# Conditioned transformer block on one core: how the ff MLP's gates reach all partitions

## The chip, the cores and the metric

The kernel runs on one core of a Trainium2 chip. The metric is the device time of one execution in microseconds. The core has five engines with a queue of instructions each: TensorE (PE in the profile, its weight loads PEld), VectorE (DVE), ScalarE (ACT), GpSimd (POOL), and SyncE (SP), which in this kernel only issues DMAs. Each works through its own queue in order, and waits where it needs another's result.

## The reference

Two batch entries of 2048 rows and 512 columns go through an MLP with exact gelu (512 to 512 to 512) and one with tanh gelu (512 to 1024 to 512). Each is wrapped in a layer norm with shift and scale, and in a gated residual sum; the six vectors (shift, scale and gate of either MLP) come from a condition, one row per batch entry.

```python
emb = jnp.dot(jax.nn.silu(t), ada_w) + ada_b            # t: (2, 512), emb: (2, 3072)
shift_msa, scale_msa, gate_msa, shift_mlp, scale_mlp, gate_mlp = jnp.split(emb, 6, axis=-1)
norm = _ln(x) * (1.0 + scale_msa[:, None]) + shift_msa[:, None]
h = jax.nn.gelu(jnp.dot(norm, ssm_w1) + ssm_b1, approximate=False)
x = x + gate_msa[:, None] * (jnp.dot(h, ssm_w2) + ssm_b2)
norm2 = _ln(x) * (1.0 + scale_mlp[:, None]) + shift_mlp[:, None]
hf = jax.nn.gelu(jnp.dot(norm2, ff_w1) + ff_b1, approximate=True)
x = x + gate_mlp[:, None] * (jnp.dot(hf, ff_w2) + ff_b2)
```

All of it is in float32. The change concerns gate_mlp, the sixth part of emb (index 5); gate_msa, the third part (index 2), is the ssm gate.

## The kernel before

**Tiling.** The 4096 rows are cut into eight blocks of 512 (128 partitions times 4 rows); blocks 0 to 3 belong to batch entry 0, blocks 4 to 7 to entry 1. Each block goes through a first product of the ssm MLP (hA_i), its second product (oA_i), a first product of the ff MLP (hC_i) and its second (oC_i).

**Products.** A product is cut into quarters and done in seven smaller products P1 to P7 in place of eight (`group`, L368 on); sums of quarters of the operands (nS, hSA, hSC, w_s, fw_s) go in, and each result is taken out of PSUM by VectorE or ScalarE. P1, P6, P7 and P4 add up in one PSUM bank (y), P5 and P3 in another (v), and P2 has a third (x). P6 may thus start only when P1's sum is taken out, P7 after P6's, P4 after P7's, P3 after P5's. The order is P1, P2, P6, P5, P7, P3, P4, in some groups with P5 ahead of P6 (`FIRST`). From block 1 on hC_i is done in 26 products of a list written out by hand (`HK_P`).

**Order.** The schedule is manual. Work of the other engines is hung as hooks behind the products of a group: each engine gets its instructions in the order in which the program issues them, and that is the order of the hooks.

**The norm's way.** x is normalized on ScalarE (`normal`, L465), turned in 32x32 squares on VectorE (`turn`, L476), moved between partitions by 16 DMAs (`move`, L485), modulated with shift and scale on ScalarE (`modulate`, L508), and its sums nS are made on GpSimd or VectorE (L311). For block 0's second norm eight of the moves are issued by SP within hA_1 and eight by ScalarE behind hA_1.

**The gates.** `rows_of_gates(g)` makes the rows of a gate for both batch entries by four column-tiled products of 512 columns (L284), one for each 128 of the 512 condition values, so that four partial sums stand in four partition groups; VectorE adds the bias row (brows) to them (L293, grows). `make_gate(g, b)` multiplies these with `pick_bc`, a matrix of ones at the rows of entry b: the product (L299, pgate) adds the four partial sums and puts the row on all 128 partitions of a PSUM tile at once. The gate is then folded into the second weight (`weight_of_second`, L359: w2 or fw2 times the gate, one of the K slices per operation) and into its bias row (gb: L830, L869, L632). The bias row is added to x on GpSimd ahead of the residual sum (`biases`, L625).

**Where the ff gate stands.** `rows_of_gates(5)` is a hook of P6 in hA_1, `make_gate(5, 0)` a hook of P3 there; gb's multiplication (gb5_0) and three of the four additions gb5 stand at P1 of oA_1, the folds of fw2 from P7 of oA_1 to hA_2. For entry 1, after oC_3, fw2 is loaded again and `make_gate(5, 1)` follows; its folds are hooks of block 4. The small loads of brows are issued on ScalarE's queue at the start, one row for each gate.

Of the kernel before, what the change touches and what calls it, by code (L numbers as in the profile page):

```python
# [36 lines left out]
F32 = mybir.dt.float32  # L37
AF = mybir.ActivationFunctionType
ALU = mybir.AluOpType
# [101 lines left out]
def kernel(  # L141
# [16 lines left out]
    nc = tc.nc  # L158
    P = 128
    B, N, D = x.shape  # L160
    H = fw1.shape[1]
    KD = D // P
    KH = H // P
    C = 4
# [3 lines left out]
    PER_B = N // TB  # L168
# [4 lines left out]
    sums = ctx.enter_context(tc.tile_pool(name="sums", bufs=4))  # L173
    work = ctx.enter_context(tc.tile_pool(name="work", bufs=1))
    small = ctx.enter_context(tc.tile_pool(name="small", bufs=3))
    ps_t = ctx.enter_context(tc.tile_pool(name="ps_t", bufs=2, space=bass.MemoryType.PSUM))
    ps_g = ctx.enter_context(tc.tile_pool(name="ps_g", bufs=2, space=bass.MemoryType.PSUM))

# [6 lines left out]
    G = 32  # L185
# [7 lines left out]
    def big_tile(name):  # L193
        return big.tile([P, KD, D], F32, tag="big", name=name)
# [9 lines left out]
    ada = {}  # L204

    def load_ada(g):
        ada[g] = big_tile(f"ada_{g}")
        nc.sync.dma_start(
            out=ada[g], in_=ada_w[:, g * D : (g + 1) * D].rearrange("(k p) n -> p k n", p=P)
        )  # L210

    def load_w(name, w, t=None, eng=nc.sync):
        if t is None:
            t = const.tile([P, w.shape[0] // P, w.shape[1]], F32, tag=name, name=name)
        eng.dma_start(out=t, in_=w.rearrange("(k p) n -> p k n", p=P))
        return t

    def load_row(t, row):
        nc.sync.dma_start(out=t, in_=row.unsqueeze(0).to_broadcast([P, D]))
        return t  # L220


    brows = big_tile("brows")
# [11 lines left out]
    w1_sb = load_w("w1", w1)  # L235
    load_ada(2)

    nc.gpsimd.memset(brows[:, :2, :], 0.0)
    for n, g in enumerate((2, 5)):
        nc.scalar.dma_start(  # L240
            out=brows[:B, n, :], in_=ada_b[g * D : (g + 1) * D].unsqueeze(0).to_broadcast([B, D])
        )
    w2_sb = load_w("w2", w2)
    b2_bc = work.tile([P, D], F32, tag="gb", name="gb2_0", bufs=2)
    load_row(b2_bc, b2)
# [4 lines left out]

    mods = {}

    def modulation(g0, part):


        g = g0 + part
        pa = ps_g.tile([P, D], F32, tag="x", name=f"pada_{g}")
        w = ada[g].rearrange("p k (n m q) -> p k m n q", n=KD, q=G)
        for k in range(KD):
            for m in range(P // G):  # L260
                nc.tensor.matmul(
                    pa[m * G : (m + 1) * G, :P],
                    silu[:, k, :],
                    w[:, k, m],
                    start=(k == 0),
                    stop=(k == KD - 1),
                    tile_position=(0, m * G),
                    skip_group_check=True,
                )
        turned = pa[:, P : 2 * P]  # L270
        nc.vector.transpose(turned, pa[:, :P])
        turned = turned.rearrange("p (n q) -> p n q", n=KD)
        m = const.tile([P, KD, B], F32, tag=f"mod_{g0}_{part}", name=f"mod_{g0}_{part}")
        bias = colsT[:, R_ADA + g * KD : R_ADA + (g + 1) * KD]
        nc.vector.tensor_tensor(m, turned[:, :, :B], bias.unsqueeze(2).to_broadcast([P, KD, B]), ALU.add)
        mods[g0, part] = m

    gate, gate_rows = {}, {}

    def rows_of_gates(g):  # L280

        pa = ps_g.tile([P, D], F32, tag="x", name=f"pada_{g}")
        for k in range(KD):
            nc.tensor.matmul(  # L284
                pa[k * G : (k + 1) * G, :],
                silu[:, k, :],
                ada[g][:, k, :],
                start=True,
                stop=True,
                tile_position=(0, k * G),  # L290
            )
        r = work.tile([P, D], F32, tag="grows", name=f"grows_{g}", bufs=2)
        nc.vector.tensor_tensor(r, pa, brows[:, (2, 5).index(g), :], ALU.add)  # L293
        gate_rows[g] = r

    def make_gate(g, b):

        pg = ps_t.tile([P, D], F32, tag="t", name=f"pgate_{g}_{b}")
        nc.tensor.matmul(pg, pick_bc[:, b, :], gate_rows[g], start=True, stop=True)  # L299
        gate[g, b] = pg  # L300


    def quarters(lo, hi, a, b):
# [36 lines left out]
    def weight_of_first(name, w_sb):  # L340

        K, M = w_sb.shape[1], w_sb.shape[2]
        tile_s = const.tile([P, 3, K // 2, M // 2], F32, tag=f"{name}_s", name=f"{name}_s")
        s = thirds(tile_s)
        lo, hi = w_sb[:, : K // 2, :], w_sb[:, K // 2 :, :]
        q = quarters(lo, hi, slice(0, M // 2), slice(M // 2, M))
        return first_operands(q, s), sums_of_first(q, s, nc.gpsimd), tile_s
# [58 lines left out]
    def hook(hooks, places, ops):  # L406

        for n, op in enumerate(ops):
            hooks.setdefault(places[min(n, len(places) - 1)], []).append(op)
# [212 lines left out]
    def biases(i, gb):  # L622

        return [
            lambda c=c: nc.gpsimd.tensor_tensor(xs[i][:, c, :], xs[i][:, c, :], gb, ALU.add)  # L625
            for c in range(C)
        ]
# [128 lines left out]
    n1 = {0: Norm(0, 1), 1: Norm(1, 1)}  # L756
# [42 lines left out]
    pick_bc = const.tile([P, B, P], F32, tag="pick_bc", name="pick_bc")  # L799
# [3 lines left out]
    w1_ops, w1_sums, _ = weight_of_first("w1", w1_sb)  # L803
# [14 lines left out]
    n1_sums = n1[0].summed(nc.vector)  # L818
    run(n1_sums[:2])
    load_ada(5)  # L820
    fw2_sb = load_w("fw2", fw2)
    gb, hA = {2: b2_bc}, {}
    found = {}

    def ssm_gate():
        make_gate(2, 0)
        found["w2"] = weight_of_second(w2_sb, w2_s, gate[2, 0], (nc.vector,))

    def gb2_0():
# [4 lines left out]

    hooks = {}
    hook(hooks, ("P1",), n1_sums[2:3])
    hook(hooks, ("P2",), [lambda: rows_of_gates(2)] + n1_sums[3:])
    st = n1[1].stats()
    hook(hooks, ("P5",), [ssm_gate, gb2_0] + biases(0, b2_bc) + fold2(0, 1))
    hook(hooks, ("P6",), fold2(1, 7))  # L840
# [5 lines left out]
    hA_sums = hA[0].summed(nc.vector)  # L846
    run(hA_sums[:2])
    hooks = {}
# [4 lines left out]
    n2 = {0: Norm(0, 2)}  # L853
    st = n2[0].stats()
    hook(hooks, ("P3",), st[:2])
    fw1_ops, fw1_sums, fw1_s = weight_of_first("fw1", fw1_sb)
# [2 lines left out]
    residual("oA_0", 0, hA[0], w2_ops, KD // 2, hooks, order=FIRST)  # L859

    def ff_gate():
        make_gate(5, 0)
        found["fw2"] = weight_of_second(fw2_sb, fw2_s, gate[5, 0], (nc.vector,), 4)

    def fold5(lo, hi):
        return [lambda k=k: found["fw2"][1][k]() for k in range(lo, hi)]
# [5 lines left out]
    n1_sums = n1[1].summed(nc.vector)  # L872
    run(st[2:3] + n1_sums[:2] + st[3:])
    hooks = {}
    hook(hooks, ("P1",), n1_sums[2:3] + [n2[0].scales])
    hook(hooks, ("P2",), n1_sums[3:] + [lambda c=c: n2[0].normal(c) for c in range(C)])
    hook(hooks, ("P2",), biases(1, gb[2]))
    hook(hooks, ("P6",), [lambda: rows_of_gates(5)])
    hook(hooks, ("P6", "P6", "P7", "P7"), [lambda c=c: n2[0].turn(c) for c in range(C)])
    hook(hooks, ("P7",), [lambda: n2[0].move((nc.sync,), (0, 1))])  # L880
    hook(hooks, ("P3",), [ff_gate])
    fb2_bc = work.tile([P, D], F32, tag="gb", name="gb5_0", bufs=2)
    load_row(fb2_bc, fb2)
    load_x(2)
# [6 lines left out]
    hA_sums = hA[1].summed(nc.vector)  # L891
# [2 lines left out]
    st = n1[2].stats()  # L894
    hooks = {}
    gb5 = biases(0, gb[5])
    hook(hooks, ("P1",), hA_sums[2:3] + [gb5_0] + fw1_sums[3:] + gb5[:3])
    hook(hooks, ("P2",), hA_sums[3:])
    hook(hooks, ("P2", "P6", "P6", "P5"), st)
    hook(hooks, ("P6",), n2[0].moved())  # L900
    n2_sums = n2[0].summed(nc.gpsimd)
    hook(hooks, ("P5",), n2_sums[:1] + [n1[2].scales])
    hook(hooks, ("P7",), n2_sums[1:] + [lambda c=c: n1[2].normal(c) for c in range(C)] + gb5[3:])
    hook(hooks, ("P7", "P3", "P4"), fold5(0, 3))
    turns = [lambda c=c: n1[2].turn(c) for c in range(C)]
    residual("oA_1", 1, hA[1], w2_ops, KD // 2, hooks)
# [2 lines left out]
    hC = Second(0)  # L909
    n2[1] = Norm(1, 2)  # L910
    hooks = {}
    hook(hooks, ("P1",), biases(2, gb[2]))
    hook(hooks, ("P1", "P1", "P2"), turns)
    hook(hooks, ("P2",), [n1[2].move])
    hook(hooks, ("P6", "P5", "P7", "P3"), n2[1].stats())
# [21 lines left out]
    hooks = {}  # L937
# [10 lines left out]
    hooks = {}  # L948
# [6 lines left out]
    hooks = {}  # L955
# [11 lines left out]
    for i in range(1, NBLK):  # L967
        nxt, nx2, last = i + 1 < NBLK, i + 2 < NBLK, i + 1 == NBLK
        hC = Second(i)
        hooks = {}  # L970
        if i == 1:
            hook(hooks, range(0, 26), take(len(fa_sums)))
        if i == 1:
            hook(hooks, (0,), [n1[i + 2].scales])
        if nxt:
            hook(hooks, (1, 2, 3, 4), hA[i + 1].summed(nc.gpsimd))
        hook(hooks, (6, 7, 8, 9), biases(i, gb[5]))
# [3 lines left out]
            hook(hooks, (20,), [n1[i + 2].move])  # L981
        if fold:
            hook(hooks, (2, 6, 23, 25), fold[:4])
        hook(hooks, (20,), hC.summed(0, nc.gpsimd))
        hC.products(fa, fb[i], hooks, last or i == 1)

        hooks = {}
# [16 lines left out]
        hooks = {}  # L1004
# [14 lines left out]
        if refold2:  # L1019
            b = (i + 2) // PER_B  # L1020
            gb[2], multiply_2 = gate_bias(2, b, b2, f"gb2_{b}")
            hook(hooks, ("P1",), [lambda: load_w("w2", w2, w2_sb)])
        if nx2:
            if refold2:
                hook(hooks, ("P1",), [lambda: make_gate(2, b)])
                hook(hooks, ("P6",), [multiply_2])
            hook(hooks, ("P1", "P2"), n1[i + 2].summed(nc.gpsimd))
            hook(hooks, ("P6",) if refold2 else ("P2", "P6"), biases(i + 2, gb[2]))
# [5 lines left out]
        if refold5:  # L1034
            b = (i + 1) // PER_B
# [22 lines left out]

        if refold5:
            load_w("fw2", fw2, fw2_sb)  # L1060
            make_gate(5, b)
            fw2_ops, fold = weight_of_second(fw2_sb, fw2_s, gate[5, b], (nc.vector,))
        hooks = {}
        if refold5:
# [51 lines left out]
```

## Time and profile before

| | |
|---|---|
| time, median of 3 runs | 600.43 us (600.42 to 600.75) |
| the profiled execution's own time | 600.48 us |
| its span, first to last instruction | 598.7 us |
| granted TensorE clock, mean | 0.999 |
| HBM read, written | 25.72 MB, 8.39 MB |
| ff gate's products, L299, each | 0.86 us on the chain, two of them |
| gate's fold of one weight slice, L359 | 0.68 us on VectorE |
| a move of nT, 64 KB, issue to landing | 2.0 us |

The span is what the profiler sees between the first and the last instruction; the execution's own time has 1.8 us more around it. In the profile's lines `out<-in` names what is written and read, and a count behind x says how many instructions a line stands for. A float32 product counts as two instructions. A wait is put down to the engine whose result came last. The chain of waits lists what released the last instruction, step by step back to the start, here in order of time. The names follow the tiles with their numbers left out: py_hA is what goes to bank y in an hA group, pada the rows of an ada product, x the residual.

### The profile page before, as it was taken

The page shows a single profiled execution, that of the slowest core. Times are in us where ns is not written, and L with a number is a line of the kernel's source. Part 1 is how long each engine was busy: PE and PEld are TensorE (multiplying, and loading weights), DVE is VectorE, ACT ScalarE, POOL GpSimd, SP SyncE. Part 2 cuts the span into 40 slices and gives each one's busy share as a digit, 9 for nine tenths or more (in the row PEclk, how much of TensorE's full clock was granted, in tenths as well). Part 3 has the DMA queues.
Part 4 walks back from the last instruction along what each step waited for, and adds up shares of the span by engine and source line. Part 5 has one row for each costly group of instructions (what it writes and reads, how often), then busy time and mean ns, then how long its engine had stood idle before and what let it go on. Part 6 is the DMA issues. An engine that isn't in the chain of part 4 may idle for free.

```text
span 598.7 us, 8148 instructions
## 1 busy us (share of the span) xinstructions
PE 591.4 (99%) x2827; PEld 510.1 (85%) x2827; DVE 374.3 (63%) x638; ACT 218.8 (37%) x363; POOL 399.1 (67%) x465
## 2 busy tenths in 40 slices
PE   8999999999999999999999999999999999999997
PEld 4787888888888888888888888888888888888886
DVE  5978988897654475555754468654565346467642
ACT  3234247305432364133721346123553225212420
POOL 2878689999743995549968498886984695540110
PEclk9999999999999999999999999999999999999999
DMA  8990222300213004340052601321020300022001
GB/s 320 412 359 10 62 68 78 102 36 36 70 72 117 25 1 121 119 129 2 14 143 65 213 8 36 106 71 71 1 65 7 106 35 1 2 58 84 0 1 70
DMA packets 23116, 49.31 MB, mean 82 GB/s; under 512 B 4340, under 2 KB 4896, under 8 KB 22180
## 3 DMA queue, kind: packets, MB, share of 16 engines
q1 hardware_dynamic: 20032, 44.58, 22.2%
q10 hardware_dynamic: 3044, 4.23, 2.7%
q8 instruction: 22, 0.36, 0.2%
q14 instruction: 18, 0.15, 0.1%
HBM read 25.72 MB, written 8.39 MB: 57 GB/s over the span
## 4 chain that ended last, share of the span: by engine, by line
PE 94%; DMA 2%; POOL 1%; DVE 1%; ACTq 1%; ACT 1%; issue 0%; SPq 0%
PE py_oC L391 18%; PE px_hC L712 10%; PE pv_oC L391 9%; PE py_hA L391 9%; PE py_oA L391 8%; PE py_hC L712 8%; PE pv_hC L712 8%; PE px_oC L391 5%; PE pv_hA L391 4%; PE pv_oA L391 4%; PE px_hA L391 2%; PE py_hC L391 2%; PE px_oA L391 2%; DMA ada<-in_L_cond_ada_w_dram 2%; PE pv_hC L391 1%; PE pt L494 1%
## 5 line engine op out<-in xcount | busy, mean ns | idle before, releaser
L625 POOL TENSOR_TENSOR x<-x,gb 128x512 f32<-128x512 f32 x64 | 79.9, 1282 | 9.3 <-DVE gb L869 3.5
L508 ACT ACTIVATE nT<-nT,mod,mod 128x512 f32<-128x512 f32 x54 | 39.6, 803 | 102.9 <-DMA nT<-blocks 102.9
L311 POOL TENSOR_TENSOR hSC<-hClo 128x512 f32<-128x512 f32 (+1 forms) x34 | 40.1, 1183 | 42.9 <-ACT hClo L707 38.7
L465 ACT ACTIVATE nT<-x,nmr,rstd 128x512 f32<-128x512 f32 x56 | 42.4, 803 | 58.4 <-POOL nmr L452 42.6
L434 POOL TENSOR_SCALAR ve<-mv 128x4 f32<-128x4 f32 x16 | 3.7, 232 | 85.8 <-DVE mv L426 85.5
L391 PE MATMUL py_oC<-fw_s,hSC 128*128 128x256 f32 x256 | 57.9, 379 | 0.0
L391 PEld LDWEIGHTS py_oC<-fw_s,hSC 128*128 128x128 f32 x256 | 48.6, 190 | 6.6
L613 DVE TENSOR_TENSOR x<-py_oC,x 128x512 f32<-128x512 f32 (+1 forms) x36 | 22.5, 629 | 40.4 <-PE py_oC L391 40.3
L425 DVE BATCH_NORM_STATS2 st<-x 128x6 f32<-128x512 f32 x64 | 43.4, 678 | 5.0 <-DMA x<-in_x_dram 4.8
L712 PE MATMUL py_hC<-forms,fw 128*128 128x256 f32 x168 | 40.8, 379 | 0.0
L476 DVE STREAM_TRANSPOSE blocks<-nT 128x512 f32<-128x512 f32 x56 | 37.8, 694 | 3.8 <-ACT nT L465 3.4
L729 DVE TENSOR_TENSOR hClo<-hClo,py_hC 128x512 f32<-128x512 f32 x42 | 28.4, 681 | 16.6 <-ACT hClo L726 10.4
L650 POOL TENSOR_TENSOR forms<-forms 128x256 f32<-128x256 f32 x48 | 35.5, 740 | 2.8
L712 PEld LDWEIGHTS py_hC<-forms,fw 128*128 128x128 f32 x168 | 31.8, 190 | 4.4
L613 DVE TENSOR_TENSOR x<-py_oA,x 128x512 f32<-128x512 f32 x32 | 22.0, 689 | 19.5 <-PE py_oA L391 19.0
L729 DVE TENSOR_TENSOR hChi<-hChi,pv_hC 128x512 f32<-128x512 f32 x35 | 23.4, 684 | 17.1 <-PE pv_hC L712 17.1
L391 PE MATMUL py_oA<-w_s,hSA 128*128 128x256 f32 x128 | 30.4, 381 | 0.2 <-DVE x L613 0.2
L391 PE MATMUL py_hA<-nS,w_s 128*128 128x256 f32 x128 | 30.4, 381 | 0.0
L707 ACT ACTIVATE hClo<-hClo,colsT 128x256 f32<-128x256 f32 x56 | 25.4, 500 | 10.8 <-DVE hClo L729 10.7
L391 PE MATMUL py_oC<-fw,hClo 128*128 128x256 f32 x128 | 28.9, 379 | 0.0
L391 PE MATMUL pv_oC<-fw,hClo 128*128 128x256 f32 x128 | 28.9, 379 | 0.0
L391 PE MATMUL pv_oC<-fw,hSC 128*128 128x256 f32 x128 | 28.9, 379 | 0.0
(210 smaller groups left out, 1405.6 us busy)
## 6 DMA issues: line engine op xcount, KB each, us to landing
nT<-blocks SPq DMA_DIRECT2D x168, 64.0 KB, 2.0
out_dram<-x SPq DMA_DIRECT2D x15, 512.0 KB, 3.2
x<-in_x_dram SPq DMA_DIRECT2D x7, 1024.0 KB, 7.3
ada<-in_L_cond_ada_w_dram SPq DMA_DIRECT2D x6, 1024.0 KB, 9.5
fw<-in_L_cond_ff_w_dram SPq DMA_DIRECT2D x3, 2048.0 KB, 9.1
nT<-blocks ACTq DMA_DIRECT2D x56, 64.0 KB, 2.0
w<-in_L_cond_ssm_w_dram SPq DMA_DIRECT2D x3, 1024.0 KB, 7.5
x<-in_x_dram SPq DMA_DIRECT2D x2, 512.0 KB, 5.1
```

Of the source, the lines that this page charges most:

```text
L311: eng.tensor_tensor(out[:, r], a[:, r], b[:, r], f)
L391: nc.tensor.matmul(ps[b][j * apart][:, j, :], lhs(p, j, k), rhs(p, j, k), start=(fresh and j * (not apart) == 0 and k == 0), stop=(p in (" ...
L425: nc.vector.bn_stats(st, xs[self.i][:, c, :])
L465: nc.scalar.activation(t, x_c, AF.Identity, bias=self.nmr[:, c : c + 1], scale=self.rstd[:, c : c + 1])
L476: nc.vector.transpose(self.bl[:, :, :, c, :].rearrange("p m k q -> p k m q"), self.nT[:, c, :].rearrange("p (k m q) -> p k m q", k=KD, m=C),)
L508: nc.scalar.activation(dst, src, AF.Identity, bias=shift, scale=scale)
L613: nc.vector.tensor_tensor(d, ps[BANK[p]][:, js], d, ALU.add)
L625: lambda c=c: nc.gpsimd.tensor_tensor(xs[i][:, c, :], xs[i][:, c, :], gb, ALU.add)
L650: eng.tensor_tensor(reg[d], reg[a], reg[b], ALU.add if f == "+" else ALU.subtract)
L707: nc.scalar.activation(h, h, AF.Gelu_apprx_tanh, bias=fb1T[:, m : m + 1])
L712: nc.tensor.matmul(ps[b][:, j, :], fa[ra][:, j * P : (j + 1) * P], fb[rb].rearrange("p a (c q) -> p c a q", q=Q), start=(fresh and j == 0) ...
L729: nc.vector.tensor_tensor(dest(d), dest(d), ps[b], op)
```

## The change

The ssm gate keeps its way (its functions are renamed). For the ff gate:
- The rows come from `rows_of(5)`, the sixteen column-tiled products of 128 columns that shift and scale already use: four partition groups hold 128 columns each, for both entries, with the condition's 512 values summed in PSUM. Its bias comes in the same layout by four small loads on SP (`load_ff_gate_b`), in place of one row on ScalarE's queue.
- Four DMAs on SP store the rows of both entries to a DRAM scratch of 2x512 values; for each entry one DMA on SP loads its row to all 128 partitions, and ScalarE copies this to the PSUM tile that the product with ones used to fill.
- Store and first load are issued at P7 of hA_1, behind SP's eight moves; the copy is a hook of P6 in oA_1, behind the four modulations. gb's multiplication goes from P1 to P7 of oA_1, the additions gb5 to the end of P7's hooks. Of the four additions of block 2's ssm bias two stay in hC_0 and two go to position 5 of block 1's products.
- Entry 1's load is a hook of position 0 of block 3's products, its copy stands where the product with ones stood.

```diff
-    for n, g in enumerate((2, 5)):
-        nc.scalar.dma_start(
-            out=brows[:B, n, :], in_=ada_b[g * D : (g + 1) * D].unsqueeze(0).to_broadcast([B, D])
-        )
+    nc.scalar.dma_start(out=brows[:B, 0, :], in_=ada_b[2 * D : 3 * D].unsqueeze(0).to_broadcast([B, D]))
+    ff_gate_b = brows[:, 1, :P]
+    def load_ff_gate_b():
+        for m in range(P // G):
+            row = ada_b[5 * D : 6 * D].rearrange("(n m q) -> m n q", n=KD, q=G)[m]
+            nc.sync.dma_start(
+                out=ff_gate_b[m * G : m * G + B, :].rearrange("p (n q) -> p n q", n=KD),
+                in_=row.unsqueeze(0).to_broadcast([B, KD, G]),
+            )
...
+    gates_dram = dram.tile([B, D], F32, tag="gates", name="gates")
+    def rows_of_ff_gate():
+        pa = rows_of(5)
+        r = work.tile([P, D], F32, tag="g5", name="grows_5", bufs=1)
+        nc.vector.tensor_tensor(r[:, :P], pa[:, :P], ff_gate_b, ALU.add)
+        gate_rows[5] = r
+    def store_ff_gates():
+        to = gates_dram.rearrange("b (n m q) -> m b n q", n=KD, q=G)
+        for m in range(P // G):
+            rows_m = gate_rows[5][m * G : m * G + B, :P].rearrange("p (n q) -> p n q", n=KD)
+            nc.sync.dma_start(out=to[m], in_=rows_m)
+    def load_ff_gate(b):
+        t = work.tile([P, D], F32, tag="g5", name=f"gsb_5_{b}", bufs=1)
+        gate_rows[5, b] = load_row(t, gates_dram[b])
+    def take_ff_gate(b):
+        pg = ps_t.tile([P, D], F32, tag="t", name=f"pgate_5_{b}")
+        nc.scalar.copy(pg, gate_rows[5, b])
+        gate[5, b] = pg
...
     fw2_sb = load_w("fw2", fw2)
+    load_ff_gate_b()
...
-        make_gate(5, 0)
+        take_ff_gate(0)
...
-    hook(hooks, ("P6",), [lambda: rows_of_gates(5)])
+    hook(hooks, ("P6",), [rows_of_ff_gate])
...
-    hook(hooks, ("P7",), [lambda: n2[0].move((nc.sync,), (0, 1))])
-    hook(hooks, ("P3",), [ff_gate])
+    hook(hooks, ("P7",), [lambda: n2[0].move((nc.sync,), (0, 1)), store_ff_gates, lambda: load_ff_gate(0)])
...
-    hook(hooks, ("P1",), hA_sums[2:3] + [gb5_0] + fw1_sums[3:] + gb5[:3])
+    hook(hooks, ("P1",), hA_sums[2:3] + fw1_sums[3:])
...
-    hook(hooks, ("P6",), n2[0].moved())
+    hook(hooks, ("P6",), n2[0].moved() + [ff_gate])
...
-    hook(hooks, ("P7",), n2_sums[1:] + [lambda c=c: n1[2].normal(c) for c in range(C)] + gb5[3:])
+    hook(hooks, ("P7",), [gb5_0] + n2_sums[1:] + [lambda c=c: n1[2].normal(c) for c in range(C)] + gb5)
...
-    hook(hooks, ("P1",), biases(2, gb[2]))
+    gb2_2 = biases(2, gb[2])
+    hook(hooks, ("P1",), gb2_2[:2])
...
+            hook(hooks, (5,), gb2_2[2:])
...
+        if (i + 1) % PER_B == 0 and nxt:
+            hook(hooks, (0,), [lambda: load_ff_gate((i + 1) // PER_B)])
...
-            make_gate(5, b)
+            take_ff_gate(b)
```

More of the change, by code (lines that the diff above doesn't have):

```diff
@@ L175 @@
     small = ctx.enter_context(tc.tile_pool(name="small", bufs=3))
+    dram = ctx.enter_context(tc.tile_pool(name="dram", bufs=1, space=bass.MemoryType.DRAM))
     ps_t = ctx.enter_context(tc.tile_pool(name="ps_t", bufs=2, space=bass.MemoryType.PSUM))
@@ L251, with rows_of @@
     mods = {}
-    def modulation(g0, part):
-        g = g0 + part
+    def rows_of(g):
         pa = ps_g.tile([P, D], F32, tag="x", name=f"pada_{g}")
@@ L269, in modulation @@
                 )
+        return pa
+    def modulation(g0, part):
+        g = g0 + part
+        pa = rows_of(g)
         turned = pa[:, P : 2 * P]
@@ L278, with rows_of_ssm_gate @@
     gate, gate_rows = {}, {}
-    def rows_of_gates(g):
-        pa = ps_g.tile([P, D], F32, tag="x", name=f"pada_{g}")
+    def rows_of_ssm_gate():
+        pa = ps_g.tile([P, D], F32, tag="x", name="pada_2")
         for k in range(KD):
@@ L286, in rows_of_gates @@
                 silu[:, k, :],
-                ada[g][:, k, :],
+                ada[2][:, k, :],
                 start=True,
@@ L291, in rows_of_gates, with make_ssm_gate @@
             )
[L292 to L300, printed above, removed]
+        r = work.tile([P, D], F32, tag="grows", name="grows_2", bufs=1)
+        nc.vector.tensor_tensor(r, pa, brows[:, 0, :], ALU.add)
+        gate_rows[2] = r
+    def make_ssm_gate(b):
+        pg = ps_t.tile([P, D], F32, tag="t", name=f"pgate_2_{b}")
+        nc.tensor.matmul(pg, pick_bc[:, b, :], gate_rows[2], start=True, stop=True)
+        gate[2, b] = pg
+    gates_dram = dram.tile([B, D], F32, tag="gates", name="gates")
[16 more added lines that the diff above has]
+        gate[5, b] = pg
     def quarters(lo, hi, a, b):
@@ L825, in ssm_gate @@
     def ssm_gate():
-        make_gate(2, 0)
+        make_ssm_gate(0)
         found["w2"] = weight_of_second(w2_sb, w2_s, gate[2, 0], (nc.vector,))
@@ L836 @@
     hook(hooks, ("P1",), n1_sums[2:3])
-    hook(hooks, ("P2",), [lambda: rows_of_gates(2)] + n1_sums[3:])
+    hook(hooks, ("P2",), [rows_of_ssm_gate] + n1_sums[3:])
     st = n1[1].stats()
@@ L1024 @@
             if refold2:
-                hook(hooks, ("P1",), [lambda: make_gate(2, b)])
+                hook(hooks, ("P1",), [lambda: make_ssm_gate(b)])
                 hook(hooks, ("P6",), [multiply_2])
```

## The prediction

> **What bounds the kernel.** I read the busy shares first, then TensorE's waits, then the chain that ended last, then single stretches. Page, part 1, and TensorE's list of waits (us in total, times, longest):
>
> ```profile
> PE 591.4 (99%) x2827; PEld 510.1 (85%) x2827; DVE 374.3 (63%) x638; ACT 218.8 (37%) x363; POOL 399.1 (67%) x465
> ```
>
> ```profile
> PE pada L261 <- DMA ada<-in_L_cond_ada_w_dram: 1.5, 2, 1.3
> PE idle L774 <- POOL ident masks.py:199: 1.3, 1, 1.3
> PE py_hC L391 <- POOL nS L311: 0.5, 1, 0.5
> PE py_oA L391 <- DVE x L613: 0.2, 1, 0.2
> PE pv_oA L391 <- DVE x L613: 0.2, 1, 0.2
> ```
>
> TensorE waits 3.7 us in all, the last time at 76.65 us; from there to the end it runs without a gap at a granted clock of 0.999. A product taken off it is a gain of its full length, if no new wait appears. Two of the waits are at the start, three between 66 and 77 us, just behind the first gate. So I follow the chain there (start us, us, what), and at the second gate:
>
> ```profile
> 52.43 0.99 PE pada L284 x8
> ...
> 57.08 0.86 PE pgate L299 x2
> 57.94 1.74 PE py_hA L391 x8
> ...
> 59.70 0.48 ACT hA L585
> ...
> 64.27 2.03 DMA nT<-blocks
> ...
> 66.56 2.94 ACT nT L508 x4
> 69.57 1.27 POOL nS L311
> ...
> 76.65 1.99 PE py_hC L391 x8
> ...
> 335.14 0.86 PE pgate L299 x2
> ```
>
> From 59.7 to 76.65 the chain leaves TensorE: ScalarE ends hA_1's last activation, issues eight moves of nT (60.4 to 64.3), the last lands at 66.3, ScalarE modulates, GpSimd forms nS, and TensorE has waited 0.48 us for it. But the chain starts at an activation that waits for the product at 57.94, and that one stands behind the gate's product.
>
> **Removed.** Two ff gate products, 0.86 us each at 57.08 and 335.14. The second stands between products that follow one another, with nothing late behind it: -0.86. The first moves the product at 57.94, the activation, ScalarE's moves, nT and nS forward by 0.86 together; SP's own eight moves (57.36 to 62.58, not shifted) land by about 64.0, before ScalarE's last at 65.4. So -0.86 as well, and the wait for nS is what is late next. The four gate row products of 512 columns (0.99 us) become sixteen of 128; the same form for ada_3 and ada_4 takes 1.01 to 1.08 us: +0.02. VectorE's addition shrinks from 0.69 us (128x512) to about 0.3 (a 128x128 transpose takes 0.33); the transposes behind it are held by the evacuation at 55.39, so this counts nothing.
>
> **Moved.** gb's multiplication (VectorE at 62.71, 0.68 us) goes from group oA_1's P1 to its P7, and the bias additions that waited for it on GpSimd (63.53 to 67.7) to behind nS's sums. VectorE gets 0.68 us earlier through there, and the sum at 63.91, which took 1.44 us beside GpSimd's additions where its fellows take 0.68, can fall to 0.7. The two waits for VectorE (0.22 and 0.21 us) go, but their gain only lengthens the wait for nS (0.48 to 0.91): nothing counted. GpSimd then has six additions of 1.25 us behind nS instead of five, ending 1.25 us later in its order, before the scales of n2_1, ahead of which it idles 2.15 us: hidden; without that cover GpSimd, busy to 138 us, would hand on 1.25 us, against a slack of 1.35 us at nS for hA_2 (ready at 99.7, read at 101.1). The two additions put off to the products of block 1 (2.5 us at about 147) meet an idle 0.85 us and then 8.79 us after the sums they delay, which oC_1 needs only from about 175: nothing.
>
> **Added at the start.** One load less on ScalarE's queue, four small ones on SP behind fw2. SP's waits show that an issue also waits for the landing of an unrelated earlier DMA: the program hands a few completion semaphores round in turn, so w1's load waits for a row load that it has nothing to do with.
>
> ```profile
> SPq L215 <- DMA brows<-in_L_cond_ada_b_dram: 2.9, 1, 2.9
> ```
>
> With one DMA fewer ahead, w1's load issues up to 0.9 us earlier (at x's landing, 4.75, not at 5.66), and its neighbours with it. They could compete with ada_1, whose landing at 11.58 releases TensorE: I bound this by 0 and 0.4 us and take 0, since ada_1 stays ahead of them on the queue. The four small loads stand ahead of x_2's (33.2), which is first read at 65.3: over 20 us to spare.
>
> **Added: the round trip of gate 0.** On SP behind its eight moves come four stores of 2x128 values and the load of one row to all partitions. Behind the load SP has only n1_2's moves (from about 77), so SP blocks nobody. The copy's own queue: ScalarE modulates nT till 68.64 (69.50 less 0.86) and next needs to work at 73.2, so a late copy holds nobody on ScalarE. On VectorE gb's multiplication waits for the copy, and behind it stand the evacuations of P3 and P4 and all of hC_0. When is the copy ready?
> - Stores: issues of 0.28 us (brows' small loads, 0.24 to 0.33) to 0.64 (the moves' pitch): the last starts between 63.5 and 64.5, take 64.0; landing 1.9 to 2.0 (out_dram, nT): 66.0.
> - Load of 256 KB: a move of 64 KB lands in 2.0, and gb2_1, the same kind of load behind eight moves, in 5.2 us:
>
> ```profile
> L219 SPq DMA_DIRECT2D gb<-in_L_cond_ssm_b_dram x1: 526/526/526, 234.7 to 234.7; - x1
> DMA to landing us min/median/max: 5.2/5.2/5.2
> ```
>
> Here nothing stands ahead or behind on the queue: I take 3.5, between the two: 69.5.
> - Copy: no copy into PSUM in this trace; ScalarE's 128x512 activations take 0.63 to 0.80. Take 0.8, ends 70.4. Bound above: a table load, 1.28 more.
>
> In this case's clock less 0.86, VectorE would come to the multiplication at 68.7. Counted forward from the copy's end at its pitch of about 0.62 us: multiplication, three folds, evacuations of P3, P4 and hC_0's P1, four transposes and P2's evacuation are 7.5 us. P6's result is there at 77.8; so a copy by 70.3 costs nothing, and the old slack of 0.44 us of P7's evacuation (83.36 against P4's start at 83.80) covers 0.4 more. **Stall = copy's end - 70.7**, never below 0: at 70.4 none, with 0.05 for the narrowness.
>
> The Trainium skill ("DMA: Bandwidth & Descriptors", Anatomy of one DMA) speaks against two small transfers in series: about 2.0 us fixed each, most of it the receipt of the write, heaviest for HBM, plus bytes over 436 GB/s (fitted for GpSimd's path). By it the load takes 2.0 + 0.6 = 2.6 us, the copy ends at 69.5, no stall, 598.8 us. By the row of 5.2 it lands at 71.2, ends at 72.05, stalls 1.35 us, 600.15. I keep 3.5, as the row had eight moves ahead of it. The same page (Rules for kernel authors, use all 16 engines) gives a transfer whose slowest dimension is 2 at most two engines; no run here shows it, and eight pieces per store leave the 1.9 us latency as the larger part.
>
> **Gate 1.** Its load issues at about 277 us and is read at 335, the copy falls where ScalarE idles 5.55 us (before 340.2), and gb's multiplication comes at 341.8: nothing.
>
> **Sum** against the profiled execution (600.48 us, span 598.7): -0.86 - 0.86 + 0.02 + 0.05 = -1.65, so 598.83. The median is 600.43, 0.05 lower: I say **598.8**, that is 0.27% less.
>
> **Rivals.**
> 1. *The first saving is swallowed*: the stores, short pieces in between ScalarE's moves, hold nT's last landing by 0.86, or the copy is up to 1.2 us late. For it: the chain from 59.7 to 76.65 is DMA latency and one queue's issues. Against it: ScalarE kept its pitch of 0.64 both beside SP's moves and after them. Left is the second gate: 600.43 - 0.84 = 599.6.
> 2. *The gate is late, and VectorE stands in front of evacuations*: slower. Place: the multiplication in P7 of oA_1; price: 1 us of TensorE for each us of landing after 69.9. At 71.5 the change is eaten up, from 72.7 it is slower by over 0.2%. If the load takes 7.1 us, as x's loads take 7.3, it lands at 73.1, the stall is 3.25: 602.0. For it: store, receipt and load are in series and none of it was on the path. Against: no idle-queue transfer of this size took so long.
> 3. *The start*: ada_1 lands 0.4 late: 599.2.
>
> **How the numbers follow.** A measurement of this kernel can tell about 0.2%, 1.2 us, from none: 599.23 to 601.63 is no change. Forecast with its small variants (rival 3 too) 0.63, rival 1 with the half-late gate 0.22, rival 2 beyond 601.6 0.15. Low end: a start 0.5 better, 598.3; high end: load at 5.2 us and the start's 0.4, 600.6.
>
> **What would show it.** No pgate product at 57 and 335; TensorE's wait for nS at 0.9 instead of 0.48; none for x at P7 and P3; the copy's end at 70 to 71; no new wait of TensorE at hC_0's P7, P3 or P4. A wait there for VectorE means rival 2; nT landing after 65.9, rival 1; ada_1 after 11.7, rival 3. I am wrong if the load takes over 5 us on an empty queue.

## The result and the profile after

The changed kernel takes 599.23 us (median of 22 runs, 598.97 to 601.29), the kernel before in the same job 600.66 us (22 runs). The ratio is 0.9976, with a 95% interval of 0.9968 to 0.9985: 0.24% or 1.4 us less, just past the bound of 0.2% that the prediction set for a change, with an interval that reaches over it; 598.8 us was predicted. The median lies about half way between the forecast and the 599.6 us of rival 1, so the time alone hardly decides between them; the product put back (below) does. Some runs of nearly every kernel here, 4 of these 22, lie about 2 us above the others with a mean granted clock of 0.997 instead of 1.0, and they are part of each median and interval.

The profiled execution took 599.55 us, its span 597.5 us against 598.7. First the busy times of the page:

```profile
PE 588.3 (98%) x2847; PEld 509.5 (85%) x2847; DVE 373.3 (62%) x638; ACT 219.9 (37%) x365; POOL 398.2 (67%) x465
```

TensorE is 3.1 us less busy, but the span is only 1.2 us shorter, so it waits more: in part at the start (2.3 us for ada in place of 1.5, and 0.7 us for brows and w, of which only 0.24 us are left at the first hA_0 product), in part in the stretch from the gate to hC_0. TensorE's timeline there (start us, us, line, what; in brackets the idle time ahead and who ended it), first a piece of the kernel before, then the changed kernel:

```profile
64.68 1.89 PE L391 MATMUL pv_oA<-w,hA 128*128 128x256 f32 x8
66.79 1.99 PE L391 MATMUL py_oA<-w_s,hSA 128*128 128x256 f32 x8 [0.22 <-DVE x L613]
68.99 1.99 PE L391 MATMUL pv_oA<-w,hSA 128*128 128x256 f32 x8 [0.21 <-DVE x L613]
70.82 1.89 PE L391 MATMUL py_oA<-w_s,hA 128*128 128x256 f32 x8
```

```profile
57.18 1.89 PE L430 MATMUL py_hA<-nS,w 128*128 128x256 f32 x8
58.90 1.89 PE L430 MATMUL py_oA<-w,hA 128*128 128x256 f32 x8
60.63 1.89 PE L430 MATMUL px_oA<-w,hA 128*128 128x256 f32 x8
62.83 1.99 PE L430 MATMUL py_oA<-w_s,hSA 128*128 128x256 f32 x8 [0.31 <-DVE hSA L350]
64.67 1.89 PE L430 MATMUL pv_oA<-w,hA 128*128 128x256 f32 x8
66.39 1.89 PE L430 MATMUL py_oA<-w_s,hSA 128*128 128x256 f32 x8
68.12 1.89 PE L430 MATMUL pv_oA<-w,hSA 128*128 128x256 f32 x8
...
76.13 1.99 PE L430 MATMUL py_hC<-nS,fw_s 128*128 128x256 f32 x8 [0.94 <-POOL nS L350]
```

The products at 66.39 and 68.12 no longer wait for x. One new wait of 0.31 us stands at 62.83, for VectorE's sums hSA: the first of them, 2.02 us long beside a sum of GpSimd, did not move forward with TensorE, nor did those behind it. It costs nothing, since it is taken out of the next wait: the wait for nS has grown from 0.48 to 0.94, as forecast. hC_0's P6 starts at 76.13 instead of 76.65.

The chain of waits of the same execution (start us, us, what) shows the round trip and the second gate:

```profile
52.68 1.01 PE pada L268 x32
...
64.76 1.62 DMA gates<-grows
...
66.50 2.58 DMA gsb<-gates
69.08 1.25 POOL nS L350
...
74.80 1.28 POOL nS L350
...
331.17 3.45 PE py_oC L430 x16
334.62 1.73 PE py_hA L430 x8
```

No ones product stands at 334. The line at 66.50 misleads: nS reads nothing of the gate. ScalarE's modulation of nT ended at that very moment (69.0), and the profile put the release down to the semaphore event that lay nearest. The copy itself tells when the gate was there (ScalarE's timeline):

```profile
66.07 2.93 ACT L547 ACTIVATE nT<-nT,mod,mod 128x512 f32<-128x512 f32 x4 [6.12 <-DMA gates<-grows]
69.79 0.59 ACT L338 COPY pgate<-gsb 128x512 f32<-128x512 f32 x1 [0.79 <-DMA gsb<-gates]
```

The copy ends at 70.38. VectorE goes on at once and stands idle again, with time to spare, at the evacuation of hC_0's P6 (0.47 us), so the gate is in time:

```profile
70.41 0.69 DVE L909 TENSOR_TENSOR gb<-pgate,gb 128x512 f32<-128x512 f32 x1 [1.26 <-ACT pgate L338]
...
78.16 0.69 DVE L604 TENSOR_TENSOR hClo<-py_hC,colsT 128x512 f32<-128x512 f32 x1 [0.47 <-PE py_hC L430]
```

### The profile page after: what moved, and what is told of

Its sections match the earlier page's. It is cut to its first block, busy times and chain, and to the rows that moved or that the text cites. A ratio compares the mean times of both kernels' runs of the same rounds, so it can differ in the third digit from the quotient of the medians.

```text
span 597.5 us, 8204 instructions
## 1 busy us (share of the span) xinstructions
PE 588.3 (98%) x2847; PEld 509.5 (85%) x2847; DVE 373.3 (62%) x638; ACT 219.9 (37%) x365; POOL 398.2 (67%) x465
## 4 chain that ended last, share of the span: by engine, by line
PE 88%; DVE 4%; DMA 3%; POOL 1%; SPq 1%; ACTq 1%; issue 1%; ACT 0%; DVEq 0%
PE py_oC L430 16%; PE px_hC L751 10%; PE py_hA L430 9%; PE py_oA L430 8%; PE pv_oC L430 8%; PE pv_hC L751 8%; PE py_hC L751 8%; PE pv_hA L430 4%; PE pv_oA L430 4%; PE px_oC L430 4%; PE px_hA L430 2%; PE py_hC L430 2%; PE px_oA L430 2%; DMA w<-in_L_cond_ssm_w_dram 2%; PE pv_hC L430 1%; ACTq L524 1%
## 5 line engine op out<-in xcount | busy, mean ns | idle before, releaser
L430 PE MATMUL py_oC<-fw_s,hChi 128*128 128x256 f32 x128 | 28.9, 379 | 0.0
```

The source lines that it names most:

```text
L430: nc.tensor.matmul(ps[b][j * apart][:, j, :], lhs(p, j, k), rhs(p, j, k), start=(fresh and j * (not apart) == 0 and k == 0), stop=(p in (" ...
```

## Experiments

All ran on the chip, four kernels to a job, each ratio against the kernel before in the same job (medians there 600.58, 600.73 and 600.62 us).

| kernel | median us | ratio to before, 95% | profiled span us | TensorE's wait ahead of hC_0's P6 |
|---|---|---|---|---|
| changed, run again | 599.56 | 0.9979 (0.9966 to 0.9992) | 597.1 | 0.96 |
| one more load at the start | 599.39 | 0.998 (0.9968 to 0.9992) | 597.3 | 1.09 |
| stores early | 601.96 | 1.0021 (1.0004 to 1.0037) | 601.8 | 2.07 |
| stores early, moves 9 to 7 | 598.61 | 0.9967 (0.9955 to 0.9979) | 596.4 | 0.28 |
| ones product at gate 0 | 600.26 | 0.9995 (0.9986 to 1.0003) | 598.1 | 1.65 |
| ones product at gate 1 | 599.98 | 0.9988 (0.9977 to 0.9999) | 597.9 | 0.97 |
| one hop more | 600.32 | 0.9997 (0.9986 to 1.0007) | 598.5 | 1.83 |
| two hops more | 605.03 | 1.007 (1.0057 to 1.0083) | 603.3 | 3.58 |
| stores early, load late | 599.03 | 0.997 (0.9958 to 0.9982) | 597.1 | 0.87 |
| the same, moves 9 to 7 | 598.51 | 0.9964 (0.9951 to 0.9976) | 596.2 | 0.25 |
| gb's work not moved | 608.0 | 1.0119 (1.0103 to 1.0134) | 605.4 | none |
| gb's work moved alone | 600.5 | 0.9996 (0.9988 to 1.0005) | 598.6 | 1.35 |

**The changed kernel again**, with no edit, and **one more load at the start**. In the profiled execution of the changed kernel the first hA_0 product started 0.24 us later than before (14.76 us), waiting for w; and 0.17 us more were lost in block 7. Theory: the DMA that ScalarE's queue no longer issues at the start shifts the loads behind it.

```diff
     nc.scalar.dma_start(out=brows[:B, 0, :], in_=ada_b[2 * D : 3 * D].unsqueeze(0).to_broadcast([B, D]))
+    nc.scalar.dma_start(out=brows[:B, 3, :], in_=ada_b[5 * D : 6 * D].unsqueeze(0).to_broadcast([B, D]))
```

> The changed kernel once more, to see what differs between two executions. Theory: the gain is two gate products, 1.72 us, less what the start costs. In the first profile after the change the start cost 0.24 us (first hA_0 product at 14.76 instead of 14.52, waiting for w1) and block 7 0.17 us (a stretched pair of products near 554). If both belong to the change, they come again: span near 597.5. If the second is chance, the span is near 597.1 to 597.3. Time 0.2 to 0.3% below before.

> The changed kernel with a second small row load put back on ScalarE's queue at the start (into an unused part of brows), so that every early load waits for the same earlier landing as in the kernel before. If the later landing of w1 comes from the shifted order of waits: w1's load issues near 5.66 again, the first hA_0 product starts at 14.5 instead of 14.76, and the time is 0.2 to 0.25 us below the changed kernel's. If it is chance or comes from elsewhere: no difference.

The first hA_0 product starts at 14.41 us in the one and 14.52 in the other, without a wait for w in either, and the times do not differ. The late start was chance of one execution, and of the loss in block 7 half came back (0.09 us): the changed kernel's span is 597.1 us as well as 597.5. The order of waits is real all the same: w1's load is issued at 5.66 us in the kernel before, at 4.63 and 4.78 in the two executions of the changed one, and at 5.66 again with the load put back. It only makes no difference to the time. A difference of 0.2 us between two profiled executions is no finding until it comes back.

The chain of the repetition also settles who releases nS:

```profile
65.73 2.94 ACT nT L547 x4
...
68.73 1.26 POOL nS L350
...
74.46 1.28 POOL nS L350
```

**Stores early**, ahead of SP's moves; then **with nine moves of nT on SP and seven on ScalarE**.

```diff
-    hook(hooks, ("P7",), [lambda: n2[0].move((nc.sync,), (0, 1)), store_ff_gates, lambda: load_ff_gate(0)])
+    hook(hooks, ("P7",), [store_ff_gates, lambda: n2[0].move((nc.sync,), (0, 1)), lambda: load_ff_gate(0)])
```

```diff
         def move(self, engs=(nc.sync,), part=range(C), rows=range(C)):
...
+    lambda: n2[0].move((nc.sync,), (2,), (0,)),
...
-    n2[0].move((nc.scalar,), (2, 3))
+    n2[0].move((nc.scalar,), (2,), (1, 2, 3))
+    n2[0].move((nc.scalar,), (3,))
```

> The changed kernel with the four stores of the gate rows ahead of SP's eight moves, where SP stands idle, and the load of gate 0 still behind them. The stores then land before the moves end, so the load issues at 62.7 instead of 66.5 and lands at 65.3 instead of 69.1; the copy is then held by ScalarE's modulations alone and ends at 69.6 instead of 70.4. Theory (the copy is within its slack, which ends near 71): no change of the time beyond 0.1 us. Rival (the copy's lateness costs part of the first saving): 0.3 to 0.8 us faster.

> As the run with the early stores, and SP issues nine of nT's sixteen moves for block 0, ScalarE seven. Theory (the wait for nS at hC_0's P6, 0.94 us, is what the first saving now stands before, and it hangs on the last issue on ScalarE's queue): the last move lands 0.5 to 0.65 us earlier, the wait shrinks to 0.3 to 0.4, the time falls by 0.5 to 0.6 us against the changed kernel. Rival (something else, as GpSimd's scales, holds nS): nothing.

The first went against both expectations, by its median slower than the kernel before; the second went as expected. The load of the gate follows SP's moves directly now, in the first at 64.05 us, just ahead of ScalarE's last two moves (64.31 and 64.95). To tell the stores' place from the load's, **stores early, load late** issues the load on ScalarE's queue behind the moves; and once more with the moves 9 to 7:

```diff
-    hook(hooks, ("P7",), [store_ff_gates, lambda: n2[0].move((nc.sync,), (0, 1)), lambda: load_ff_gate(0)])
+    hook(hooks, ("P7",), [store_ff_gates, lambda: n2[0].move((nc.sync,), (0, 1))])
...
     n2[0].move((nc.scalar,), (2, 3))
+    load_ff_gate(0, nc.scalar)
...
```

> The kernel with the early stores, but with the load of gate 0 issued on ScalarE's queue behind its eight moves of nT instead of on SP's queue ahead of their landing. If the early stores lost their time because the row load (256 KB) runs beside ScalarE's last moves: the last move of nT lands about 1.7 us after its issue ends, as in the changed kernel, and not 2.9; TensorE's wait for nS is 0.9 to 1.0 us instead of 2.07; time within 0.3 us of the changed kernel run again (ratio 0.998 to the kernel before). If it is the stores' place ahead of SP's moves itself that costs, the wait stays near 2 us and the time near the kernel before's (ratio 1.000 to 1.002).

> The same, with nine moves of nT on SP and seven on ScalarE. One issue less on ScalarE's queue lets nT land some 0.6 us earlier: wait for nS 0.3 us, ratio 0.9965 to 0.997 to the kernel before, as with the split and the load on SP (0.9967). If the row load also disturbs the moves in the split kernel, up to 0.3 us better than that, no wait for nS left.

The chain with the load on SP's queue, then with the load behind the moves:

```profile
64.95 3.26 DMA nT<-blocks
...
68.48 2.94 ACT nT L547 x4
...
78.54 1.67 PE py_hC L430 x6
```

```profile
63.51 2.06 DMA nT<-blocks
...
65.83 2.94 ACT nT L548 x4
...
75.88 1.99 PE py_hC L431 x8
```

The last move of nT takes 3.26 us where it stands beside the 256 KB load and 2.06 where the load follows it (2.03 in the kernel before). That is 1.2 us at the place where everything waits for nT. The delay is in the transfer: the packets of ScalarE's queue, which here carries only those moves, end between 67.5 and 68.0 us, over 2.5 us behind the last issue, against between 65.5 and 66.0, at most 1.7 us behind it (64.27), in the kernel before. In the kernel with the moves 9 to 7 the same load starts 0.35 us behind ScalarE's last issue (63.13 against 62.78) and stretches nothing: there those packets end by 64.5. The early stores themselves cost nothing. In the profiled execution with the load on SP's queue two stretches of lower clock come on top (window; its length, then busy time and instructions of PE, PEld, DVE, ACT and POOL; TensorE's granted clock; DMA share, GB/s):

```profile
12.00:16.00 4.00, 4.00 (x48) 3.53 (x41) 1.15 (x3) 1.00 (x2) 1.39 (x2) 0.62 1.05 406
16.00:20.00 4.00, 4.00 (x22) 3.03 (x24) 3.80 (x5) 1.84 (x2) 3.84 (x3) 1.00 1.07 395
78.00:82.00 4.00, 3.46 (x11) 2.89 (x12) 2.89 (x6) 2.78 (x4) 3.92 (x4) 0.73 0.09 20
82.00:86.00 4.00, 4.00 (x17) 3.39 (x17) 3.12 (x8) 0.00 (x0) 4.00 (x5) 0.84 0.41 102
```

Behind the wait of 2.07 us two groups take 5.6 us instead of 3.9. What the second stretch adds (1.7 us) follows from the longer wait; the first, at the start, is no part of the edit. The timed executions show that neither comes always: the mean granted clock was 0.999 or 1.0 in four of the twelve (600.13 to 600.56 us), 0.997 in four (601.91 to 602.27) and 0.994, as in the profiled one, in four (603.76 to 604.46). So the load beside the moves costs some 0.9 us against the changed kernel's executions at full clock (median 599.42 in this job); what the median of 601.96 has beyond that, and with it the place behind the kernel before, is lost clock.

Both kernels with the moves 9 to 7 beat the kernel before: 598.61 and 598.51 us, 0.33% and 0.36% less. Against the changed kernel their intervals overlap, but the wait for nS is down from 0.96 us to 0.28 and 0.25, and the profiled spans, 596.4 and 596.2 us against 597.1, agree with that. Their own difference is not resolved.

**Each saving put back**: one unread ones product in hA_1's P3, or behind oC_3, where the gates' products were.

```diff
+    def ones_product(name):
+        pg = ps_t.tile([P, D], F32, tag="t", name=name)
+        nc.tensor.matmul(pg, pick_bc[:, 0, :], gate_rows[2], start=True, stop=True)
...
+    hook(hooks, ("P3",), [lambda: ones_product("extra_0")])
```

> The changed kernel with one product with ones put back, unread, in the place of the first gate's (ahead of P3 and P4 of hA_1, 0.86 us of TensorE). Theory (the first saving passes through the moves of nT and the wait for nS): about +0.86 us against the unchanged kernel run again (599.56 us median, profiled span 597.1), the wait for nS still 0.9 to 1.0 us, hC_0's P6 0.86 later. Rival 1 (the saving is swallowed by the moves or the late gate): +0 to +0.2, and the wait for nS shrinks by 0.86 to about 0.1.

> The changed kernel with one unread product with ones put back in the place of the second gate's (about 334 us, between products that follow one another). Theory: TensorE runs without a gap from 76 us to the end, so +0.86 us against the unchanged kernel run again, all of it still there at the end. If the later blocks take part of a shift back or add to it, it is +0.6 or +1.1 instead.

TensorE's waits with the product at gate 0:

```profile
PE pada L268 <- DMA ada<-in_L_cond_ada_w_dram: 2.0, 2, 1.5
PE py_hC L434 <- POOL nS L354: 1.6, 1, 1.6
```

Had the saving been swallowed, the wait for nS would have shrunk by 0.86 us. It grew by 0.7: nT and nS come later by all of the product, by 0.13 us by which that execution began later, and by 0.15 us more in the moves (ScalarE's modulation starts at 66.87 instead of 65.73), while TensorE makes good a part, as the 0.31 us wait for hSA is gone. P6 starts 1.17 us later, the span is 1.0 us longer, and by the ratios the product costs 0.16% or 0.96 us. So the first saving does pass through the moves. The second costs 0.8 us of span and 0.5 us by the ratios, whose intervals are wide enough for 0.86 in both cases.

**The gate made late**: one and two more copies DRAM to DRAM between the stores and the load of gate 0.

```diff
...
-        gate_rows[5, b] = load_row(t, gates_dram[b])
+        src = gates_dram
+        if b == 0:
+            for hop in (hop_0, ):
+                nc.sync.dma_start(out=hop, in_=src)
+                src = hop
+        gate_rows[5, b] = load_row(t, src[b])
```

> The changed kernel with one more copy DRAM to DRAM between the stores of the gates and the load of gate 0: the load is issued some 2 us later, the copy on ScalarE ends at about 72.3 instead of 70.2. By the prediction's rule (stall = copy's end less 70.7) 1.6 us, by the slack left in the trace of after (0.47 us of VectorE ahead of the evacuation of hC_0's P6 and 0.31 at P4's start, so the stall begins at a copy's end of about 71.2) 1.1 us: +1.1 to +1.6 against the changed kernel run again, and TensorE waits for VectorE in hC_0 at P7, P3 or P4. Rival: the gate has more slack than that (+0), the waits of TensorE stay as they were.

> The same with two copies DRAM to DRAM in series: the copy on ScalarE ends at about 74.4. Stall by the prediction's rule 3.7 us, by the slack of the trace of after 3.2: that much over the changed kernel run again, some 602.8, slower than before; and 2.1 us over the kernel with one such copy if TensorE pays 1 us for each us of lateness. If a TensorE that stands idle for 2 us or more also loses clock, as the run with the early stores hints, 0.5 to 1.5 us more and a granted clock under 0.95 in the 20 us behind the wait.

TensorE's timeline with one hop, then with two:

```profile
76.70 1.97 PE L436 MATMUL py_hC<-nS,fw_s 128*128 128x256 f32 x8 [1.83 <-DVE hClo L610]
78.51 1.89 PE L436 MATMUL pv_hC<-nT,fw 128*128 128x256 f32 x8
```

```profile
79.12 3.75 PE L437 MATMUL py_hC<-nS,fw_s 128*128 128x256 f32 x8 [3.58 <-DVE hClo L611]
82.67 3.14 PE L437 MATMUL pv_hC<-nT,fw 128*128 128x256 f32 x8
85.64 1.89 PE L437 MATMUL py_hC<-nS,fw_s 128*128 128x256 f32 x8
```

With one hop the copy ends at 72.25, and P6 waits for VectorE's evacuation where it had waited for nS: 0.87 us more, and the products behind it lose 0.6 us more in that execution; 1.1 us by the ratios. With two the copy ends at 74.67. The wait is 2.6 us over that for nS, less than the 3.2 to 3.7 expected; but the two groups behind it take 6.9 us in place of 3.9. The table by stretches says why, first one stretch behind the wait of 1.83 us with one hop, then the kernel with two:

```profile
78.00:82.00 4.00, 4.00 (x20) 3.20 (x18) 3.96 (x8) 0.63 (x1) 4.00 (x4) 1.00 0.13 33
```

```profile
74.00:78.00 4.00, 1.54 (x8) 1.01 (x6) 3.30 (x6) 3.91 (x6) 3.84 (x4) 1.00 0.00 0
78.00:82.00 4.00, 2.88 (x7) 2.38 (x8) 3.97 (x7) 1.46 (x2) 4.00 (x4) 0.54 0.01 4
82.00:86.00 4.00, 4.00 (x13) 3.23 (x12) 2.20 (x5) 0.00 (x0) 3.15 (x3) 0.60 0.32 79
86.00:90.00 4.00, 4.00 (x21) 3.51 (x20) 3.93 (x9) 0.63 (x1) 0.00 (x0) 1.00 0.40 101
```

Here too the clock is lower behind the wait, about halved for most of eight microseconds: 3.0 us on top. All five timed executions with two hops had a mean granted clock of 0.994. After the wait of 1.83 us it stays at 1.00. So two hops cost 5.5 us by the ratios, not the 3.2 to 3.7 of the rule: the wait is shorter than the rule has it, and the lost clock, which the rule leaves out, is more than that difference.

**gb's work not moved**: copy, gb's multiplication and the additions back in oA_1's P1.

```diff
-    hook(hooks, ("P1",), hA_sums[2:3] + fw1_sums[3:])
+    hook(hooks, ("P1",), hA_sums[2:3] + [ff_gate, gb5_0] + fw1_sums[3:] + gb5[:3])
...
-    hook(hooks, ("P6",), n2[0].moved() + [ff_gate])
+    hook(hooks, ("P6",), n2[0].moved())
...
```

> The changed kernel with the copy, gb's multiplication and the bias additions of block 0 back in P1 of oA_1 (and the additions of block 2 back in P1 of hC_0), as in the kernel before. VectorE then stands still in P1 from about 62 us until the copy has ended (70), with the evacuations of P1, P2 and P6 behind it. Theory: TensorE waits about 6 us in oA_1, and after so long a wait its clock falls for some 4 us more: 605 to 609 us in all, slower by 1 to 1.5%. Rival: the copy, now ahead of nT's modulation on ScalarE, also shifts that, and only the later of the two counts: 603 to 605. If the move of these operations is not needed, it is within 0.3 us of the changed kernel.

TensorE, in its timeline:

```profile
64.48 1.89 PE L430 MATMUL pv_oA<-w,hA 128*128 128x256 f32 x8
74.01 3.52 PE L430 MATMUL py_oA<-w_s,hSA 128*128 128x256 f32 x8 [7.64 <-DVE x L652]
77.36 1.89 PE L430 MATMUL pv_oA<-w,hSA 128*128 128x256 f32 x8
```

VectorE stands still for 7.37 us ahead of the multiplication, with two evacuations behind it, and TensorE for 7.64. With 1.6 us of lost clock in the next group, less the wait for nS of 0.96 that is covered, that is 8.3 us; the spans differ by 8.3. The round trip pays only because the work that needs it was put eight microseconds later.

**gb's work moved alone**, in the kernel before, with its products with ones:

```diff
-    hook(hooks, ("P1",), hA_sums[2:3] + [gb5_0] + fw1_sums[3:] + gb5[:3])
+    hook(hooks, ("P1",), hA_sums[2:3] + fw1_sums[3:])
...
-    hook(hooks, ("P7",), n2_sums[1:] + [lambda c=c: n1[2].normal(c) for c in range(C)] + gb5[3:])
+    hook(hooks, ("P7",), [gb5_0] + n2_sums[1:] + [lambda c=c: n1[2].normal(c) for c in range(C)] + gb5)
...
-    hook(hooks, ("P1",), biases(2, gb[2]))
+    gb2_2 = biases(2, gb[2])
+    hook(hooks, ("P1",), gb2_2[:2])
...
+            hook(hooks, (5,), gb2_2[2:])
```

> The kernel before with the products, and only gb's multiplication and the bias additions moved as in the change. Prediction: no change (ratio 0.9995 to 1.0005): TensorE's two waits of 0.2 us for VectorE in oA_1 go, and the wait for nS grows by as much, from 0.5 to 0.9. Rival: GpSimd, free earlier, brings nS forward, or its additions behind nS are late for n2_1's scales: 0.4 us either way (0.9993 or 1.0007).

```profile
PE pada L261 <- DMA ada<-in_L_cond_ada_w_dram: 2.1, 2, 1.6
PE py_hC L391 <- POOL nS L311: 1.3, 1, 1.3
PE idle L774 <- POOL ident masks.py:199: 1.3, 1, 1.3
```

Those are all of TensorE's waits: both for x are gone, and the time is that of before. P6 starts at 76.59 instead of 76.65. The wait for nS, however, grew by 0.87, not by the 0.43 that the two waits showed. Both are right: in the kernel before, the groups at those waits follow one another by 2.11 and 2.20 us and the next by 1.83 (the four lines of the kernel before, further up), where 1.73 is the pitch without a wait.

## Why the prediction was right

- **The two products**, -0.86 each: shown for the first (0.96 us by the ratios, 1.0 us of span), and for the second with less certainty (0.5 and 0.8). Rival 1, the swallowed saving, is refuted, as the wait for nS grew with the product put back. A trace of it is there, which the sum had at nothing: seven of ScalarE's moves take 4.58 to 4.62 us of its queue where the stores run beside them, and 4.44 to 4.47 where they don't (the kernel before, gb's work moved alone, and two kernels with the stores early), so the stores hold nT back by 0.1 us, not by 0.86.
- **The rows**: 1.01 us for the 32 instructions against 0.99, the 0.02 foreseen.
- **The moved operations**: nothing, shown by moving them alone. The size of what moves into the wait for nS was too small (0.87 us, not 0.43); that the 0.94 us of the changed kernel met the forecast of 0.91 was luck, because the new wait for hSA took some of it back. GpSimd's six additions are hidden: 0.92 us are left ahead of n2_1's scales, where 2.15 us stood.
- **The copy's end**, 70.4 foreseen and 70.38 measured, was partly luck. The last store started at 64.76 instead of 64.0, since the stores took 0.59 to 0.71 us of the queue each, at the upper end of the range taken and over it; the load was issued at 66.50 instead of 66.0. From there to the copy's start it took 3.29 us (3.06 to 3.34 in the kernels with the load on SP and no overlap), close to the 3.5 taken between the rows and above the 2.6 estimated from the Trainium skill ("DMA: Bandwidth & Descriptors", Anatomy of one DMA); and the copy took 0.59 us, not 0.8.
- **Stall = copy's end less 70.7**: the cause is right (VectorE's evacuations in hC_0), the place only in part, and the onset nearly. The prediction counted to the evacuation of P6's result and named P7, P3 and P4 for the wait; but P6 itself may start only when P1's sum is taken out, which is VectorE's seventh operation behind the copy, and there the wait of 1.83 us fell, with 0.6 us more at P3 and P4. Subtracting the added wait from the copy's end gives an onset of 71.4 at P6 with one hop and 71.3 with two (that execution began 0.7 us later), and 70.8 with all 1.5 us of the execution with one hop. The slack of 0.44 us at P4 is 0.30 by TensorE's timeline (its start there is 83.66, not 83.80); nothing hung on it.
- **Rival 2's price**, 1 us for each us of lateness, holds only for a short wait. By it a copy 4.6 us later than in the repetition costs 4.0 us; two hops cost 5.5 by the ratios and 6.2 of span, 3.0 of it lost clock. So 602.0 us was too low for a gate as late as that rival had it, and the risk on that side was underestimated.
- **The start**: nothing, as taken, though w1's load did go out about 1 us earlier, as worked out; ada_1's products began at 11.63 instead of 11.62, so rival 3 did not come.
- **The sum**: -1.65 us against a measured -1.4 (0.9 to 1.9 by the interval). The 1.2 us of the profiled pair is less, for 0.24 us at the start, which did not come back, and 0.17 us in block 7, of which half did; the repetition's span is 1.6 us shorter than before.

## What to carry to other kernels

Follow a removed instruction through the engines that it lets start earlier: the first product was worth its length though TensorE waits behind it, because the wait's own chain began behind the product. A round trip through DRAM in place of a TensorE product is free only where its consumer stands later than store, load and copy together, here some eight microseconds; and what else runs on the transfers' path matters more than the queue's order, as one row load beside the last moves of nT cost 1.2 us. When such a trip could make TensorE wait for two microseconds or more, price the lost clock as well as the wait.

## What was unexpected of the hardware

- **The clock behind a wait.** TensorE's granted clock stayed at 1.00 after a wait of 1.83 us, fell to 0.73 and 0.84 in two stretches of 4 us after one of 2.07, and to 0.54 and 0.60 after one of 3.58, which cost 1.7 and 3.0 us. The losses have one size: what the clock lacks of 1.00 adds up to 1.7 us behind the wait of 2.07, to 1.7 again at that execution's start (0.05 and 0.38 of 4 us), and to 3.4, twice that, behind the wait of 3.58, where part of it fell in the wait itself. One such loss is 0.003 of the span, and so fits the mean clock of 0.997, two fit 0.994. The Trainium skill ("TensorE: Matmul & The Clock Gate", Part 1: The HAM clock gate) gives half clock after an idle window of about 3.4 us. By it alone the wait of 2.07 us would be free; in the one execution profiled it was not. It does not always cost: of the twelve timed executions four lost no clock, and the four at 0.994 lost it twice. In the four at 0.997 it is open whether the loss stood at the start or behind the wait.
- **A short wait costs more than it shows**: waits of 0.22 and 0.21 us delayed their groups by 0.38 and 0.47 us against the pitch of 1.73.
- **A small store is not a cheap issue**: 1 KB in short pieces holds SP's queue for 0.59 to 0.71 us, as long as a move of 64 KB (0.53 to 0.60).
